# Attention beside a mixture of experts on one core: choice weights at step 70, block experts ten steps behind the slots, pairs sent at two places of a step, biases as bf16 rows of the projection

## The chip, the cores and the metric

The kernel runs on one core of one Trainium2 chip. Five engines work side by side, each through its own instructions in order: PE (TensorE, matmuls; its weight loads are shown as PEld), DVE (VectorE), ACT (ScalarE), POOL (GpSimd) and SP (which issues DMAs). The metric is the device time of one execution in microseconds (us), the median over several; lower is better.

## The reference

Input x is 8 x 512 tokens of 128 features. Both branches read the layer-normed x, and the output is their sum with x:

```python
xn = layernorm(x)
# attention, 16 heads of 8
h = xn @ W1 + b1                       # q, k, v
w = softmax(causal(q k^T / sqrt(8)))
attn = (w @ v) @ Wp + bp
# mixture of 8 experts, 2 per token, and one shared
logits = xn @ gate_w.T
topw, topi = top_k(softmax(logits), 2)
topw = topw / (topw.sum(-1) + 1e-20)
ffn(x, g, u, d) = silu(x @ g.T) * (x @ u.T) @ d.T     # 352 wide
moe = ffn(xn, shared) + sum over i of topw[i] * ffn(xn, expert[topi[i]])
out = x + attn + moe
```

## The kernel before

PE, DVE, ACT and SP work in the order in which the program was written; only POOL's instructions are put in order by a scheduler. The main loop (L1153) goes over 32 groups of four heads (eight batches of four groups), with five tiles of scores each: 160 steps. A step fills one PSUM tile with scores (`fill`, L315, single-buffered), takes the exponential on ACT (`weigh`, pT L443, 128x1024), and looks seven tiles ahead (`look`, L740): PE computes raw scores into two PSUM banks (sc_diag, sc_left, L365) and DVE reduces them to row maxima (peaks L394, L400), which are turned (mT L423, L425) and written by DMA as rows beside the queries. In `MORE` = steps 0, 12, 18, 24 the step looks twice, the second time at its end (L1182). Where `prepare` (L350) ran before a look, ACT has copied the causal mask into sc_diag (L353); where it has not, PE adds it by a matmul of 128x512 bf16 (L378).

Beside the scores, each step runs pieces of the expert network (`chunk`, L600): gu matmuls (L611), tanh on ACT (L616), two DVE operations that end in the gated h (L617, L618), and later the down projection y (L638). Shared blocks of 256 tokens come first (13 of them, to step 41), then 36 blocks of routed pairs, then the last shared ones. A shared block adds its y to x_sb on DVE (L648); a routed one copies it on ACT (o L644) and POOL scatters it (results L622).

Routing runs inside the same steps, one piece of the generator `route` (L907) per step from step 0 on: maxima of the logits and the places of all 8192 token-choice pairs (slot L986, step 5), the expert of each block (L991 to L998, step 6), and the choice weights (L1005 to L1023, step 7). From step 5, `send_some` (L682) issues two indirect DMAs per step on POOL (slots L690), each moving 128 rows to their slots; both wait for the exponential of their step. There are 64, and the slots are first loaded at step 40 and used at step 41. The weights are first used when the routed results are added, after step 148.

`offset` (L526) adds the sum of projected v bias and bp (bias_sb, made in `whole_bias`, L517) to a batch's x_sb on POOL (L529, 128x512), eight times in all. `join` (L533) projects a batch's attention with four fp32 matmuls (p_ps L537) and adds it to x_sb (L541). Two PSUM buffers named "mi" are shared in turn by all small results: v_ps, mT_ps, y, s_ps, ot, p_ps and others, so a new one waits until the one before the last has been read.

The order within a step, from the loop:

```python
waiting.append((kind, j, weigh(n, kind, j, on_pool)))
parts_then = look(step)
some_chunks(step, False)
...
parts_then()
if step not in MORE and len(looked) < total_steps:
    prepare(*divmod(len(looked), NTILES))
some_routing()
send_some()
```

Of the kernel before, what the change touches and what calls it, by code (L numbers as in the profile page):

```python
# [11 lines left out]
F32 = mybir.dt.float32  # L12
I32 = mybir.dt.int32
BF16 = mybir.dt.bfloat16
# [11 lines left out]
P = 128  # L26
# [26 lines left out]
AT_ONCE = 2  # L53
SENT = 2
LAG = 2
# [10 lines left out]
def attn_moe_kernel(  # L66
# [34 lines left out]
    bp_sb = const.tile([P, E], F32, name="bp_sb")  # L101
    bias_sb = const.tile([P, E], F32, name="bias_sb")

    def load_x(b):
# [91 lines left out]
    rows = rows_attT[:, :, :E]  # L196
    attT = rows
    weight = const.tile([P, TOPK, NT], F32, name="weight")
    slot = const.tile([P, TOPK, NT], I32, name="slot")
# [236 lines left out]

    last_exp = []

# [86 lines left out]

    def offset(b):  # L526
        xb = x_sb[:, ts(b, NC), :]
        with tc.issue_after(sent[-1]) if sent else ExitStack():
            nc.gpsimd.tensor_tensor(  # L529
                xb, xb, bias_sb.unsqueeze(1).to_broadcast([P, NC, E]), ALU.add  # L530
            )

    def join(b):  # L533

        ps = misc([P, NC, E], "p_ps")
        for c in range(NC):
            nc.tensor.matmul(  # L537
                ps[:, c], lhsT=attT[:, b * NC + c], rhs=wp_sb, start=True, stop=True
            )
        xb = x_sb[:, ts(b, NC), :]  # L540
        nc.vector.tensor_tensor(xb, ps, xb, ALU.add)  # L541
# [58 lines left out]
    def chunk(k, f):  # L600
# [16 lines left out]
        nc.vector.scalar_tensor_tensor(th, th, 1.0, gu[:, 0], ALU.add, ALU.mult)  # L617
        nc.vector.tensor_tensor(h[:, f], gu[:, 1], th, ALU.mult)  # L618

# [68 lines left out]
    def send(i, t):  # L688

        d = nc.gpsimd.indirect_dma_start(  # L690
            slots, bass.IndirectOffsetOnAxis(ap=slot[:, i, t : t + 1], axis=0),
            rows_attT[:, t, :], None,
        )
# [96 lines left out]
    nc.gpsimd.tensor_copy(count, count_i)  # L790
    logits = ro.tile([P, NT, NE], F32, name="logits")
    empty = ro.tile([P, WIPED, ROW], F32, name="empty")
# [114 lines left out]
    def route():  # L907

        rank_b = rank.unsqueeze(1).to_broadcast([P, NT, NE])
        lmax = ro.tile([P, NT], F32, name="lmax")  # L910
        nc.vector.tensor_reduce(lmax, logits, AX.X, ALU.max)
# [3 lines left out]
        for i in range(TOPK):  # L915
            if i:
                rest = ro.tile([P, NT, NE], F32, name="rest")
                nc.vector.scalar_tensor_tensor(rest, hots[0], MASKED, logits, ALU.mult, ALU.add)
                left = rest
                top = ro.tile([P, NT], F32, name=f"top{i}")  # L920
                nc.vector.tensor_reduce(top, left, AX.X, ALU.max)
# [65 lines left out]
        to_send.extend((i, t) for t in range(NT) for i in range(TOPK))  # L987
        yield

# [10 lines left out]
        )  # L1000
        yield


        prob = ro.tile([P, NT, NE], F32, name="prob")
        nc.vector.tensor_tensor(prob, logits, spread(lmax), ALU.subtract)  # L1005
        nc.scalar.activation(prob, prob, AF.Exp)
        psum = ro.tile([P, NT], F32, name="psum")
        nc.vector.tensor_reduce(psum, prob, AX.X, ALU.add)
        nc.vector.reciprocal(psum, psum)
        chosen = []  # L1010
        for i in range(TOPK):
            p_ = ro.tile([P, NT], F32, name=f"p{i}")
            nc.vector.tensor_tensor(p_, tops[i], lmax, ALU.subtract)
            nc.scalar.activation(p_, p_, AF.Exp)
            nc.vector.tensor_tensor(p_, p_, psum, ALU.mult)
            chosen.append(p_)
        wsum = ro.tile([P, NT], F32, name="wsum")
        nc.vector.scalar_tensor_tensor(
            wsum, chosen[0], 1e-20, chosen[1], ALU.add, ALU.add
        )  # L1020
        nc.vector.reciprocal(wsum, wsum)
        for i in range(TOPK):
            nc.vector.scalar_tensor_tensor(  # L1023
                weight[:, i], chosen[i], 0.5, wsum, ALU.mult, ALU.mult
            )

    routing = route()
    done_routing = []

# [81 lines left out]
    for t in range(FIRST):  # L1111
# [17 lines left out]
        if t == 3:  # L1129
            whole_bias()  # L1130
            offset(0)
        if t == 4:
# [20 lines left out]
    for n in range(B * NG):  # L1153
        b, g = divmod(n, NG)
        waiting = []
        for i, (kind, j) in enumerate(TILES):
# [13 lines left out]
            some_routing()  # L1170
            send_some()
            for f in late:
# [116 lines left out]
```

## Time and profile before

| what | us |
|---|---|
| three timed runs | 618.37, 620.67, 620.8 |
| median | 620.67 |
| the profiled execution | 616.3 |
| its span, first to last instruction | 614.6 |
| mean granted clock of PE | 0.968 of full |

The profile is of one execution. Its busy times are unions over an engine's instructions; an idle time is put down to whatever semaphore event came last before the waiting instruction. Matmul ends are modelled.

| group of instructions | count | mean ns |
|---|---|---|
| exponential, ACT L443, 128x1024 | 160 | 1026 |
| row maxima, DVE L394, 128x512 | 256 | about 684 |
| gu, PE L611, shared, 128x256 fp32 | 192 | 406 |
| mask into sc_diag, ACT L353 | 117 | 592 |
| mask matmul, PE L378, 128x512 bf16 | 11 | 381 |
| send of pairs, POOL L690 | 64 | 979 |
| bias added to x_sb, POOL L529 | 8 | 1271 |

Idle time of PE, DVE and ACT by what ended it is read from the list of waits; where in the run it falls, from the timeline.

### The profile page before, as it was taken

How to read it: one execution, taken by the hardware profiler on the slowest of the kernel's cores; microseconds unless marked ns; L12 is line 12 of the kernel's file. 1: busy time of each engine (PE TensorE's matmuls, PEld its weight loads, DVE VectorE, ACT ScalarE, POOL GpSimd, SP SyncE). 2: the span in 40 equal slices, each digit the busy share in tenths (PEclk: the TensorE clock that was granted, in tenths of full speed). 3: DMA queues.
4: the chain of work that ended last, by engine and by line, in shares of the span. 5: the costliest groups of instructions: out<-in, count | busy, mean ns of one | idle time of the engine just before them, and what ended most of it. 6: DMA issues, size and time to landing. Idle time of an engine off the chain costs nothing.

```text
span 614.6 us, 13602 instructions
## 1 busy us (share of the span) xinstructions
PE 563.3 (92%) x4796; PEld 414.0 (67%) x4796; DVE 463.3 (75%) x1213; ACT 370.4 (60%) x668; POOL 244.0 (40%) x365
## 2 busy tenths in 40 slices
PE   6989598798999999999999999999999999999964
PEld 4656375566666677777776877777777877786533
DVE  7787867676768787777787778687788778876594
ACT  5735354463547666686667666586667766665530
POOL 9510444643557234333433344233434334433320
PEclk9989799998999999999999999999999999999986
DMA  7744244142143674838585785838585875720471
GB/s 219 229 117 172 95 109 109 37 131 78 37 121 110 197 225 135 233 106 251 178 240 159 223 233 166 217 93 250 178 218 194 238 232 145 215 96 3 138 223 51
DMA packets 52363, 98.38 MB, mean 160 GB/s; under 512 B 10054, under 2 KB 35530, under 8 KB 50136
## 3 DMA queue, kind: packets, MB, share of 16 engines
q1 hardware_dynamic: 46216, 83.78, 47.6%
q0 software_dynamic: 5360, 13.66, 6.4%
q8 instruction: 38, 0.62, 0.4%
q14 instruction: 29, 0.24, 0.1%
q10 hardware_dynamic: 720, 0.08, 0.1%
HBM read 73.36 MB, written 24.26 MB: 159 GB/s over the span
## 4 chain that ended last, share of the span: by engine, by line
PE 67%; ACT 6%; DVE 6%; issue 2%; POOL 0%; ACTq 0%; DVEq 0%
PE gu L611 19%; PE av L466 11%; PE y L638 11%; PE scT L322 9%; PE sc_diag L365 5%; PE sc_left L365 4%; DVE x_sb L719 3%; ACT pT L443 2%; PE qk_ps L239 2%; ACT sc_diag L353 2%; PE p_ps L537 1%; ACT th L616 1%; PE s_ps L585 1%; PE aT_ps L514 1%; PE mT_ps L423 1%
## 5 line engine op out<-in xcount | busy, mean ns | idle before, releaser
L443 ACT ACTIVATE pT<-scT 128x1024 f32<-128x1024 f32 x160 | 164.1, 1026 | 68.6 <-PE scT L322 27.3
L622 POOL DMA_INDIRECT results<-o,goes x72 | 73.1, 1015 | 129.7 <-ACT o L644 110.0
L451 POOL TENSOR_SCALAR_AFFINE_SELECT pT<-pT 128x256 f32<-128x256 f32 (+1 forms) x168 | 72.4, 447 | 118.7 <-ACT pT L443 115.6
L611 PE MATMUL gu<-sT,w 128*128 128x128 f32 x864 | 116.0, 277 | 2.3 <-PE sc_left L365 0.8
L394 DVE TENSOR_REDUCE peaks<-sc_diag 128x4 f32<-128x512 f32 x128 | 88.0, 688 | 38.1 <-PE sc_diag L365 25.7
L611 PEld LDWEIGHTS gu<-sT,w 128*128 128x128 f32 x864 | 108.0, 191 | 6.8 <-PE sc_diag L365 1.8
L322 PE MATMUL scT<-qs,ks 75*128 75x384 bf16 (+3 forms) x512 | 103.2, 303 | 3.9 <-ACT pT L443 3.8
L690 POOL DMA_INDIRECT slots<-rows_attT,slot x64 | 62.6, 979 | 81.2 <-issue 36.2
L616 ACT ACTIVATE th<-gu 128x256 f32<-128x256 f32 x156 | 59.8, 384 | 57.7 <-PE gu L611 39.7
L466 PE MATMUL av<-pT,v_ext 128*32 128x512 f32 (+3 forms) x1024 | 91.2, 452 | 1.0 <-POOL pT L451 1.0
L365 PEld LDWEIGHTS <-qs 72*128 72x128 bf16 x896 | 64.9, 98 | 38.8 <-issue 20.6
L617 DVE SCALAR_TENSOR_TENSOR th<-th,gu 128x256 f32<-128x256 f32 x156 | 65.1, 417 | 32.7 <-ACT th L616 30.5
L394 DVE TENSOR_REDUCE peaks<-sc_left 128x4 f32<-128x512 f32 x128 | 87.1, 680 | 0.0
L353 ACT CAST sc_diag<-mask_q 128x512 f32<-128x512 bf16 x117 | 69.2, 592 | 25.3 <-DVE peaks L394 17.9
L365 PE MATMUL sc_diag<-ks,qs 72*128 72x128 bf16 (+1 forms) x576 | 62.1, 225 | 12.4 <-ACT sc_diag L353 11.0
L618 DVE TENSOR_TENSOR h<-gu,th 128x256 f32<-128x256 f32 x156 | 66.2, 424 | 5.4
L638 PEld LDWEIGHTS y<-w,h 128*128 128x128 f32 x432 | 54.2, 191 | 23.4 <-issue 10.6
L638 PE MATMUL y<-w,h 128*128 128x128 f32 x432 | 64.4, 285 | 1.2 <-ACT v_ext L289 1.2
L365 PE MATMUL sc_left<-ks,qs 72*128 72x128 bf16 (+1 forms) x320 | 61.7, 274 | 3.2 <-DVE peaks L394 3.1
L322 PEld LDWEIGHTS <-ks 75*128 75x128 bf16 x512 | 46.8, 99 | 23.7 <-issue 12.5
L611 PE MATMUL gu<-xnT,ws_sb 128*128 128x256 f32 x192 | 54.1, 406 | 3.3 <-DVE h L618 3.2
L466 PEld LDWEIGHTS av<-pT,v_ext 128*32 128x32 f32 x1024 | 23.6, 109 | 32.2 <-issue 21.6
(166 smaller groups left out, 634.5 us busy)
## 6 DMA issues: line engine op xcount, KB each, us to landing
w<-in_w_exp_dram SPq DMA_DIRECT2D x72, 576.0 KB
qs<-dq SPq DMA_DIRECT2D x45, 192.0 KB
ks<-dk SPq DMA_DIRECT2D x45, 192.0 KB
slots<-empty POOLq DMA_DIRECT2D x6, 780.0 KB
s<-slots SPq DMA_DIRECT2D x33, 130.0 KB
r<-results SPq DMA_DIRECT2D x16, 256.0 KB
dq<-parts SPq DMA_DIRECT2D x7, 384.0 KB
dk<-parts SPq DMA_DIRECT2D x7, 384.0 KB
```

Of the source, the lines that this page charges most:

```text
L322: nc.tensor.matmul(out_, lhsT=k[: QK + 3, ts(i, P)], rhs=q[: QK + 3, i * P :], start=True, stop=bare)
L353: nc.scalar.copy(diag_ps.rearrange("p (b k) -> p b k", k=P), mask_q.unsqueeze(1).to_broadcast([P, NC, P]),)
L365: nc.tensor.matmul(out_, lhsT=q[:QK, ts(c, P)], rhs=k[:QK, keys], start=start, stop=stop, skip_group_check=True,)
L394: nc.vector.tensor_reduce(peaks[:, i, 8 + 4 * t : 12 + 4 * t], banks[t].rearrange("p (b k) -> p b k", k=P), AX.X, ALU.max,)
L443: last_exp[:] = [nc.scalar.activation(pT, ps, AF.Exp, scale=D**-0.5).ins]
L451: nc.gpsimd.affine_select(out=d, in_=d, pattern=[[0, d.shape[1]], [1, P]], compare_op=ALU.is_ge, fill=0.0, base=0, channel_multiplier=-1,)
L466: nc.tensor.matmul(av[32 * jj : 32 * jj + 32, c * P :], lhsT=v_ext[b % NV][:, c, 4 * g + jj, :], rhs=weights, start=(n % 2 == 0 and c == 0 ...
L611: nc.tensor.matmul(gu[:, i, part], lhsT=w[c][:, ds(i * FP + f * P, P)], rhs=sT[:, part], start=True, stop=True,)
L616: nc.scalar.activation(th, gu[:, 0], AF.Tanh, scale=0.5)
L618: nc.vector.tensor_tensor(h[:, f], gu[:, 1], th, ALU.mult)
L622: d = nc.gpsimd.indirect_dma_start(results, bass.IndirectOffsetOnAxis(ap=goes_of[k][:, c : c + 1], axis=0), o, None, bounds_check=NP - 1, ...
L638: nc.tensor.matmul(y, lhsT=h[:, f, ts(c, P)], rhs=w[c % len(w)][:, ds(2 * FP + f * P, P)], start=(f == 0), stop=(f == NF - 1),)
```

## The change

Five edits. The block experts follow the slots by ten steps (`EXPERTS_AT`), at step 15. The choice weights become a generator of their own, run from step 70 to 73 (`WEIGHTS_AT`), with their inputs (logits, maxima) kept in buffers that live through the kernel. Of the two sends of a step the second is issued at its end and waits for the gated h of the step's chunk instead of the exponential. In steps 13, 19 and 25 the chunk stands ahead of the look, and the mask is no longer prepared by ACT for them. `offset` goes; the sum of biases is split into three bf16 parts, each kept on one row of a 128x128 tile, and a matmul with ones adds these rows in `join`.

```diff
-SENT = 2
+EXPERTS_AT = 10
+WEIGHTS_AT = 70
...
     def whole_bias():
...
+        part = ln.tile([P, 3, E], BF16, name="bias_part", bufs=1)
+        for i in range(3):
+            nc.gpsimd.tensor_copy(part[:, i], bias_sb)
+            if i < 2:
+                nc.gpsimd.tensor_tensor(bias_sb, bias_sb, part[:, i], ALU.subtract)
+            nc.gpsimd.tensor_scalar(
+                part[:, i], part[:, i], ident[:, i : i + 1], None, ALU.mult
+            )
+        nc.gpsimd.tensor_tensor(bias16, part[:, 0], part[:, 1], ALU.add)
+        nc.gpsimd.tensor_tensor(bias16, bias16, part[:, 2], ALU.add)
-    def offset(b):
-        xb = x_sb[:, ts(b, NC), :]
-        with tc.issue_after(sent[-1]) if sent else ExitStack():
-            nc.gpsimd.tensor_tensor(
-                xb, xb, bias_sb.unsqueeze(1).to_broadcast([P, NC, E]), ALU.add
-            )
     def join(b):
...
-                ps[:, c], lhsT=attT[:, b * NC + c], rhs=wp_sb, start=True, stop=True
+                ps[:, c], lhsT=attT[:, b * NC + c], rhs=wp_sb, start=(c == 0), stop=False,
+                skip_group_check=True,
             )
+        nc.tensor.matmul(
+            ps, lhsT=ones16, rhs=bias16.unsqueeze(1).to_broadcast([P, NC, E]),
+            start=False, stop=True, skip_group_check=True,
+        )
...
-        nc.vector.tensor_tensor(h[:, f], gu[:, 1], th, ALU.mult)
+        last_gate[:] = [nc.vector.tensor_tensor(h[:, f], gu[:, 1], th, ALU.mult).ins]
...
-    def send_some():
-        for _ in range(SENT):
-            if to_send:
-                send(*to_send.pop(0))
+    def send_one(behind):
+        if to_send:
+            send(*to_send.pop(0), behind)
...
-        tc.add_manual_dep(d.ins, last_exp[0].name, SYNC, reason="in their step")
+        tc.add_manual_dep(d.ins, behind.name, SYNC, reason="in their step")
...
         to_send.extend((i, t) for t in range(NT) for i in range(TOPK))
-        yield
+        for _ in range(EXPERTS_AT):
+            yield
...
+    def weigh_choices():
+        nc.vector.tensor_tensor(logits, logits, spread(best[0]), ALU.subtract)
+        nc.scalar.activation(logits, logits, AF.Exp)
+        chosen = best[2:]
+        for p_, top in zip(chosen, best):
+            nc.vector.tensor_tensor(p_, top, best[0], ALU.subtract)
+            nc.scalar.activation(p_, p_, AF.Exp)
         yield
-        prob = ro.tile([P, NT, NE], F32, name="prob")
-        nc.vector.tensor_tensor(prob, logits, spread(lmax), ALU.subtract)
-        nc.scalar.activation(prob, prob, AF.Exp)
...
+        nc.vector.tensor_reduce(best[1], logits, AX.X, ALU.add)
+        nc.vector.reciprocal(best[1], best[1])
+        yield
+        for p_ in chosen:
+            nc.vector.tensor_tensor(p_, p_, best[1], ALU.mult)
...
+        yield
...
             whole_bias()
-            offset(0)
...
-            parts_then = look(step)
-            some_chunks(step, False)
+            if step - 1 in MORE:
+                some_chunks(step, False)
+                parts_then = look(step)
+            else:
+                parts_then = look(step)
+                some_chunks(step, False)
...
             some_routing()
-            send_some()
+            if step >= WEIGHTS_AT:
+                next(weighing, None)
+            send_one(last_exp[0])
...
             some_chunks(step, True)
+            send_one((last_gate or last_exp)[0])
+            last_gate.clear()
             if step in MORE:
                 look(step)()
-                prepare(*divmod(len(looked), NTILES))
...
-        if n % NG == 2 and b + 1 < B:
-            due(step + 1, partial(offset, b + 1))
```

On the engines' orders this means: PE gains eight bias matmuls (and two mask matmuls, in steps 13 and 25), ACT loses two mask copies, POOL gains ten small operations in the preamble and loses eight additions, DVE's instructions are the same and stand elsewhere, and SP's order is the same.

More of the change, by code (lines that the diff above doesn't have):

```diff
@@ L102, in attn_moe_kernel @@
     bias_sb = const.tile([P, E], F32, name="bias_sb")
+    bias16 = const.tile([P, E], BF16, name="bias16")
     def load_x(b):
@@ L197, in attn_moe_kernel @@
     attT = rows
+    logits = const.tile([P, NT, NE], F32, name="logits")
+    best = []
+    for i in range(2 * TOPK):
+        t = const.tile([P, NT], F32, name=f"best{i}")
+        best.append(t)
     weight = const.tile([P, TOPK, NT], F32, name="weight")
@@ L435, in put_shift @@
             )
-    last_exp = []
+    last_exp, last_gate = [], []
     def weigh(n, kind, j, on_pool):
@@ L680, in attn_moe_kernel, with send @@
     to_send = []
-    def send_some():
-        for _ in range(SENT):
-            if to_send:
-                send(*to_send.pop(0))
-    def send(i, t):
+    def send_one(behind):
+        if to_send:
+            send(*to_send.pop(0), behind)
+    def send(i, t, behind):
         d = nc.gpsimd.indirect_dma_start(
@@ L790, in attn_moe_kernel @@
     nc.gpsimd.tensor_copy(count, count_i)
-    logits = ro.tile([P, NT, NE], F32, name="logits")
     empty = ro.tile([P, WIPED, ROW], F32, name="empty")
@@ L909, in route @@
         rank_b = rank.unsqueeze(1).to_broadcast([P, NT, NE])
-        lmax = ro.tile([P, NT], F32, name="lmax")
+        lmax = best[0]
         nc.vector.tensor_reduce(lmax, logits, AX.X, ALU.max)
@@ L919, in route @@
                 left = rest
-                top = ro.tile([P, NT], F32, name=f"top{i}")
+                top = best[i]
                 nc.vector.tensor_reduce(top, left, AX.X, ALU.max)
@@ L1000, in route @@
         )
-        yield
-        prob = ro.tile([P, NT, NE], F32, name="prob")
[L1005 to L1017, printed above, removed]
+    def weigh_choices():
[5 more added lines that the diff above has]
+            nc.scalar.activation(p_, p_, AF.Exp)
+        yield
+        nc.vector.tensor_reduce(best[1], logits, AX.X, ALU.add)
[3 more added lines that the diff above has]
+            nc.vector.tensor_tensor(p_, p_, best[1], ALU.mult)
         nc.vector.scalar_tensor_tensor(
-            wsum, chosen[0], 1e-20, chosen[1], ALU.add, ALU.add
+            best[0], chosen[0], 1e-20, chosen[1], ALU.add, ALU.add
         )
-        nc.vector.reciprocal(wsum, wsum)
+        yield
+        nc.vector.reciprocal(best[0], best[0])
         for i in range(TOPK):
             nc.vector.scalar_tensor_tensor(
-                weight[:, i], chosen[i], 0.5, wsum, ALU.mult, ALU.mult
+                weight[:, i], chosen[i], 0.5, best[0], ALU.mult, ALU.mult
             )
     routing = route()
+    weighing = weigh_choices()
     done_routing = []
```

## The prediction

> **What bounds the kernel now.** I read the page first, then the sums by stretch, the waits of PE, and the timeline at each wait. "Step" is one pass of the inner loop, found in the trace by its exponential (pT L443, 160 of them).
>
> ```profile
> PE 563.3 (92%) x4796; PEld 414.0 (67%) x4796; DVE 463.3 (75%) x1213; ACT 370.4 (60%) x668; POOL 244.0 (40%) x365
> ...
> 61.00:85.40 24.40, 17.90 (x120) 12.54 (x119) 17.29 (x49) 9.46 (x20) 10.25 (x10) 0.79 0.42 116
> 85.40:126.00 40.60, 34.88 (x287) 23.95 (x286) 29.48 (x74) 21.05 (x34) 20.67 (x21) 1.00 0.24 66
> ...
> 201.00:304.30 103.30, 99.92 (x909) 77.06 (x906) 81.22 (x205) 69.81 (x131) 38.05 (x62) 1.00 0.66 194
> ```
>
> In a row by stretch, the first pair is start:end, then length, busy time of PE, PEld, DVE, ACT, POOL, then the granted clock. From 201 us on PE is busy 97%: that stage is bound by PE's own instructions. From 61 to 126 us (steps 6 to 19) PE idles 12.2 of 65 us, and in the first part its clock is 0.79. That early stage is what can be won. Its waits, from the timeline (start, duration, engine, line, and in brackets the idle time before it and what ended it):
>
> ```profile
> 71.76 0.42 ACT L1006 ACTIVATE prob<-prob 128x256 f32<-128x256 f32 x1 [1.13 <-DVE prob L1005]
> ...
> 73.68 0.23 ACT L1014 ACTIVATE p<-p 128x32 f32<-128x32 f32 x1 [0.36 <-DVE p L1013]
> 73.81 0.63 ACT L289 COPY v_ext<-v_ps 128x256 f32<-128x256 f32 x2
> ...
> 74.50 1.65 PE L638 MATMUL y<-ws_sb,h 128*128 128x128 f32 x6 [3.43 <-ACT v_ext L289]
> ...
> 97.39 0.38 PE L365 MATMUL sc_diag<-ks,qs 72*128 72x128 bf16 x4 [1.80 <-ACT sc_diag L353]
> ...
> 121.19 0.38 PE L365 MATMUL sc_left<-ks,qs 72*128 72x256 bf16 x2 [1.54 <-DVE peaks L394]
> ...
> 147.30 0.38 PE L365 MATMUL sc_diag<-ks,qs 72*128 72x128 bf16 x4 [2.22 <-ACT sc_diag L353]
> ```
>
> The choice weights (L1005 to L1025) bounce between DVE and ACT; the v copy queued behind them on ACT comes 2.9 us after its v_ps ended (70.90), and PE stands 3.43 us for the buffer. The other three waits are in the steps after those that look twice (MORE: 12, 18, 24). Two waits lie elsewhere:
>
> ```profile
> 102.87 0.97 POOL L690 DMA_INDIRECT slots<-rows_attT,slot  x1 [0.30 <-issue]
> ...
> 104.89 1.02 ACT L443 ACTIVATE pT<-scT 128x1024 f32<-128x1024 f32 x1 [2.64 <-PE gu L611]
> 104.93 0.69 DVE L400 TENSOR_REDUCE peaks<-sc_left 128x2 f32<-128x512 f32 x1 [1.77 <-PE gu L611]
> ...
> 205.12 1.27 POOL L529 TENSOR_TENSOR x_sb<-x_sb,bias_sb 128x512 f32<-128x512 f32 x1 [2.71 <-DVE second L588]
> 205.13 1.27 DVE L592 SCALAR_TENSOR_TENSOR goes<-second,s 128x2 int32<-128x2 f32 x1
> ```
>
> ACT and DVE start together at 104.9, though PE had issued the scores they need by 103.3: what PE finished was told late. It is 1.0 us after the end (103.84) of the last of four indirect sends in a row (99.03, 100.30, 101.59, 102.87). The same holds for the rows of four that end at 94.82 and 144.72 (DVE's x_sb L648 starts at 95.82 and 145.74). I read it as: after four sends back to back PE's signals are held for about 1 us; rows of two show no clear hold.
>
> **What the Trainium skill says.** "TensorE: Matmul & The Clock Gate", What's actually happening: PE's clock is full or half, decided over windows of about 3.4 us of activity. The trace agrees: PE is at half clock from 72.9 to 79.7 and 148.0 to 151.4, each right after an idle of 3.43 and 2.22 us; idles of 1.8 us and less brought none. "SBUF — State Buffer", SBUF: two separate sides: GpSimd and VectorE share a port pair as an exclusive lock, and a VectorE operation with two SBUF inputs waits for the whole GpSimd one. The trace agrees: goes L592 (mean 193 ns) took 1.27 us beside the POOL addition of the same length. On sends that hold PE's signals I found no page.
>
> **The change part by part**, against the profiled execution (span 614.6 us, 616.3 in all). The median of the three timed runs is 620.67, 4.4 above it; I take the differences over to the median.
>
> *Weights to steps 70 to 73, experts ten steps later.* Step 6 loses four DVE instructions (66.73 to 68.61: 1.9 us), step 7 eleven on DVE and three on ACT (71.31 to 75.1). Re-laying ACT and DVE there: parts L254 starts at 66.85, the reductions at 67.7, the v copy at 70.95 when v_ps is done, so y L638 starts at 71.65 instead of 74.50: 2.85. With an idle of 0.6 instead of 3.43 the half-clock window goes too; PE's work from 74.5 to 79.9 then takes 5.4 - 2.6. By the end of step 8's gu I get 74.8 for 79.92: **-5.0** (-2.9 if the half clock stays). Next late is again the ACT copy of the mask, 0.3 as before. In step 15 the experts' 1.9 us land on DVE at 108.1, where DVE stood idle for 2.1 us waiting on POOL's offset (x_sb L648, 110.23), so they take that gap.
>
> At step 70 (304.3) the cost comes back in a PE-bound stage: DVE gets three operations after h (306.9), ACT three exponentials behind them, ahead of o_sb, sT and the next exponential. Laid out, ACT is free at about 308.3, so o_sb starts 1.9 us late, PE's ot waits 0.8 for it, and the next scores 0.35 for the exponential: **+1.2**. Steps 71 to 73 add only DVE work of 0.5 to 0.8 us before waits of 0.6 to 1.2. Bounds 0 and +2.1 (the whole ACT delay).
>
> *Chunk before look in steps 13, 19, 25, no mask copied for them.* gu (0.9 to 1.03) runs in the wait; in 13 and 25 the mask comes as a matmul (L378, next instruction 0.22 later) instead of an ACT copy of 0.59. Without a held signal as well, the reductions are done when gu is: step 13 -1.8 + 0.2 = **-1.6**, step 19 **-1.0**, step 25 -2.2 + 0.2 = **-2.0**, and its half-clock window, 3.4 us, goes: **-1.7**.
>
> *Sends at two places.* The second now waits for the gate (h L618) of its step. Laying the 64 sends out by the ends of exponentials and gates in this trace, rows of four in steps 8 to 27 vanish (longest there three); some remain at steps 30 to 36, where the present ones cost PE little (0.7 at 174.5, 0.8 at 182.9). Gain in step 15: DVE's chain runs from 103.4, x_sb at 108.8 for 110.23: **-1.4** (-0.2 if the hold stays). Steps 28 to 35: **-0.5** (0 to -1.5). Behind a waiting send stand on POOL only later sends; the last one ends where it did (190.3 in both layouts), and the loads of slots behind them lose three offsets of 1.27.
>
> *Biases in the projection.* Eight POOL additions go; one of them held goes L592 1.1 us and through ACT's v copy PE's s_ps (wait 1.37 at 208.3): **-1.05**. Eight matmuls of 128x512 bf16 come, at the 0.22 us of L378's form: **+1.8** (0 if they fall in waits; 3.0 at the 381 ns each takes alone). At the start ten POOL operations of 128x128 stand at 29 to 33 us, some with two SBUF inputs, beside DVE's small m_parts chain; with the fetch landing late anyway I take **+0.3** (0 to +1).
>
> Sum: -5.0 - 1.6 - 1.0 - 3.7 - 1.4 - 0.5 - 1.05 = -14.25; +1.2 + 1.8 + 0.3 = +3.3; together **-11.0**. All of the gain lies before the PE-bound stage, which then starts earlier; the SP order is the same, weights and slots are triggered by step, and the row maxima that SP loads for the scores have 6.5 us or more from issue to use (95.97 to 102.44, the shortest after step 6). So 605.3 for the profiled execution, and 609.7 for the median, 610 rounded.
>
> **Rivals.**
> A (0.60): as laid out, 610; own range 606 to 614.
> B (0.22): the send layout doesn't help, because gate and next exponential come close together and rows of four persist in other steps. For it: the steps get shorter, and gate to exponential is often under 1.27 us. Against: my layout. Then step 13 gives 0.8, step 15 0.2, step 25 2.5, the late part 0: -7.3, 613.4.
> C (0.11): the early stage is refilled: another wait, DVE's (busy 71 to 73% there) or the fetches of q and k, takes the freed time, and of 14.25 only some 5 remain: -1.7, 619.
> D (0.07), slower: the exchange in steps 70 to 73 and the bias matmuls at their high ends (2.1 + 3.0 + 1 = 6.1) while the second send, waiting at the head of POOL's queue for gates, delays the last slots. Today these loads are issued at 197.1 to 199.4 and first used by PE at 203.4. From about 3 us of delay on, PE stands at step 41, each such idle of over 2.2 us brings a half-clock window, and it decides once more than 8 us are lost there. Then 624. Against it: the layout ends at the same place.
>
> **Numbers.** Three us (0.5%) is about what a measurement of this kernel tells from no change. Faster by more (under 617.6): all of A and B and a little of C, 0.84; the same: most of C, 0.09; slower: D, 0.07. Range 605.5 to 616.5: A and B with the bounds of the half clock (2.1), the late sends (1.0) and step 70 (1.2), C and D left out.
>
> **What would show it.** Weights: no ACT wait at L1006's place, y L638 of step 7 within 1 us of v_ps, clock of the stretch from 69 to 80 us at 1.0. Chunks: no wait over 0.6 us before sc_diag in steps 13 and 25. Sends: no start of ACT and DVE together 1 us after a fourth send. Bias: matmuls of 128x512 bf16 0.22 apart. Step 70: ot waiting for o_sb by 0.5 to 1.5 us. Wrong if PE idles as much before 200 us as now, or if slots come late at step 41.

## The result, and the profile after

The changed kernel took 610.28 us (median of 4 runs, 609.00 to 612.92), the kernel before 619.52 (4 runs, 617.86 to 620.8; three of them are the runs shown before the prediction): ratio 0.9858, 95% interval 0.9813 to 0.9902, a gain of 6.1 to 11.6 us. Some executions have a lower clock and lie over 1.5% above the fastest of their kernel; the medians here and below count them and the ratios leave them out, so a ratio need not be the quotient of its medians. The profiled execution of the changed kernel took 609.89 us with a span of 608.2; that of the kernel before had 616.3 and 614.6.

First the engines' totals and the sums by stretch of the changed kernel (start:end, length, then busy time of PE, PEld, DVE, ACT, POOL, the granted clock, DMA share and GB/s):

```profile
PE 564.8 (93%) x4806; PEld 412.0 (68%) x4806; DVE 460.8 (76%) x1213; ACT 368.2 (61%) x666; POOL 236.9 (39%) x367
...
61.00:80.00 19.00, 15.36 (x117) 10.37 (x116) 13.55 (x35) 9.25 (x17) 9.57 (x10) 0.91 0.46 127
80.00:119.00 39.00, 36.03 (x298) 24.96 (x297) 30.98 (x79) 20.29 (x33) 19.43 (x21) 1.00 0.29 79
...
191.00:294.00 103.00, 100.68 (x914) 77.73 (x913) 80.45 (x205) 69.78 (x131) 35.55 (x60) 1.00 0.65 195
```

The two early stretches cover the same steps (6 to 19) as before. They are 58 us long for 65, PE idles 6.6 us in them for 12.2, and the clock of the first has gone from 0.79 to 0.91. The PE-bound stage is as full as it was.

Now the waits that the prediction had named, from the timeline of the changed kernel (start, duration, engine, line, in brackets the idle time before it and what ended it):

```profile
72.31 0.94 PE L655 MATMUL y<-ws_sb,h 128*128 128x128 f32 x6 [0.57 <-ACT v_ext L297]
...
94.24 0.38 PE L373 MATMUL sc_diag<-ks,qs 72*128 72x128 bf16 x4 [0.65 <-ACT sc_diag L361]
...
107.95 0.96 POOL L706 DMA_INDIRECT slots<-rows_attT,slot  x1 [0.30 <-issue]
...
109.83 0.69 DVE L402 TENSOR_REDUCE peaks<-sc_diag 128x4 f32<-128x512 f32 x1 [2.35 <-PE gu L628]
...
114.72 0.38 PE L373 MATMUL sc_left<-ks,qs 72*128 72x256 bf16 x2 [1.54 <-DVE peaks L402]
...
139.04 0.39 PE L373 MATMUL sc_diag<-ks,qs 72*128 72x128 bf16 x4
...
161.69 0.96 POOL L706 DMA_INDIRECT slots<-rows_attT,slot  x1 [0.30 <-issue]
...
163.87 1.02 ACT L451 ACTIVATE pT<-scT 128x1024 f32<-128x1024 f32 x1 [2.95 <-PE gu L628]
```

Step 7's wait for the copy of v fell from 3.43 to 0.57 us. Of the waits after a double look, that of 1.80 in step 13 and that of 2.22 in step 25 (139.04 has no bracket) are gone; the 0.65 at 94.24 stands one step later, at the look of step 14, whose mask ACT still copies. That of 1.54 at step 19 is there as before. The last send shown ends a row of four at 162.65, and ACT's exponential starts 1.2 us after it: PE's signals are still held, here and at 108.91, where a row of three ended. ("Held" means that ACT or DVE starts late on something that PE had finished.)

One wait that the prediction did not list is as long as before and now the longest of this stage: at 66.41 in the changed kernel, ahead of the look of step 7, PE stands 2.79 us for ACT's copy of the mask (2.78 in the kernel before), and a half-clock window follows, from 67.0 to 70.4. e7 and f2 below try to shorten it.

The table follows the start of the exponential step by step, changed minus before, in us, as what each stretch of steps added. The first column is this pair of traces; the second is the pair e6 and e5 below, from a chip on which the kernel before takes 609 us.

| steps | first pair | e5 minus e6 |
|---|---|---|
| to 5 | +0.69 | +0.01 |
| 6 to 9 | -5.38 | -4.55 |
| 10 to 14 | -1.35 | -0.19 |
| 15 to 19 | -1.19 | +0.33 |
| 20 to 24 | +0.43 | -0.33 |
| 25 to 27 | -3.68 | -0.60 |
| 28 to 41 | +0.75 | 0.00 |
| 42 | -1.06 | -1.07 |
| 43 to 69 | +0.45 | +0.46 |
| 70 to 73 | +0.89 | +0.89 |
| 74 to 159 | +4.4 | -2.3 |

The last row is no work of the change except the 0.21 to 0.25 us of each of four projections before the last steps. In the first pair the rest stands from step 148 on, beside half-clock windows (before 588 to 592 and 599 to 602, after 555 to 559 and 582 to 589); in the second, 2.97 of it stand at step 130, in a half-clock window that e6 alone has, from 499 to 503. These windows differ between executions of one kernel. "TensorE: Matmul & The Clock Gate" of the Trainium skill, What's actually happening, calls the window free-running and what it costs run-variable; these traces agree: the changed kernel's second trace (e5) has none between 71 and 592 us.

### The profile page after: what moved, and what is told of

The parts are those of the page before. It is cut to its first block, busy times and chain, and to the rows that moved or that the text cites. A ratio compares the mean times of both kernels' runs of the same rounds, so it can differ in the third digit from the quotient of the medians.

```text
span 608.2 us, 13658 instructions
## 1 busy us (share of the span) xinstructions
PE 564.8 (93%) x4806; PEld 412.0 (68%) x4806; DVE 460.8 (76%) x1213; ACT 368.2 (61%) x666; POOL 236.9 (39%) x367
## 4 chain that ended last, share of the span: by engine, by line
PE 76%; DVE 9%; ACT 8%; issue 3%; DMA 2%; SPq 0%; POOL 0%; ACTq 0%; DVEq 0%; POOLq 0%
PE gu L628 21%; PE av L474 12%; PE y L655 12%; PE scT L330 10%; PE sc_diag L373 6%; PE sc_left L373 5%; ACT pT L451 3%; DVE x_sb L735 3%; PE qk_ps L247 2%; ACT sc_diag L361 2%; DVE peaks L402 2%; ACT th L633 2%; PE p_ps L549 1%; PE s_ps L602 1%; DVE h L635 1%
## 5 line engine op out<-in xcount | busy, mean ns | idle before, releaser
L639 POOL DMA_INDIRECT results<-o,goes x72 | 72.9, 1012 | 131.4 <-ACT o L661 110.0
L330 PEld LDWEIGHTS <-ks 75*128 75x128 bf16 x512 | 46.6, 99 | 23.5 <-issue 12.2
```

Of the source, the lines that this page charges most:

```text
L330: nc.tensor.matmul(out_, lhsT=k[: QK + 3, ts(i, P)], rhs=q[: QK + 3, i * P :], start=True, stop=bare)
L639: d = nc.gpsimd.indirect_dma_start(results, bass.IndirectOffsetOnAxis(ap=goes_of[k][:, c : c + 1], axis=0), o, None, bounds_check=NP - 1, ...
```

## The experiments

Times are medians of 6 to 22 runs; ratios are to the kernel before, run on the same chip. e1 to e4 ran on one chip, e5 to e8 on a second, f1 to f3 on a third and g1 on a fourth, each on one occasion; which chip the first pair ran on is not on record.

**e1, both sends at one place.** The changed kernel with

```diff
             send_one(last_exp[0])
+            send_one(last_exp[0])
...
-            send_one((last_gate or last_exp)[0])
-            last_gate.clear()
```

> The changed kernel, but both sends of a step stand at one place behind the exponential, as before the change. Theory (rows of four sends back to back hold PE's signals for about 1 us): rows of four come back in steps 8 to 27; exponentials start later than in the changed kernel by 0.8 at step 13, 1.2 more at step 15 and 0.5 to 2.5 more at step 25; in all +2 to +4.5 us, ratio to the kernel before 0.989 to 0.993. Rival (the place of the second send doesn't matter, the hold follows the number of sends that fall near each other in any layout): within 1 us of the changed kernel, ratio 0.985 to 0.987, and no new wait of PE over 0.5 us in steps 8 to 27.

604.92 us, ratio 0.9914 (0.9889 to 0.9939). But the kernel before, 619.5 the first time, took 610.33 here, and the ratios expected for e1 to e4 were worked out from 619.5. So I compare these four with e5 below, the changed kernel beside a kernel before of 609.37; that e1's ratio lies in the theory's range says nothing. By the ratios e1 is 0.7 us slower than e5 (the two intervals leave -1.6 to 2.9). In the timeline of e1 the rows of four are back, and nothing is held:

```profile
142.14 0.96 POOL L706 DMA_INDIRECT slots<-rows_attT,slot  x1 [1.69 <-ACT pT L451]
...
145.93 0.95 POOL L706 DMA_INDIRECT slots<-rows_attT,slot  x1 [0.31 <-issue]
...
146.90 0.22 PE L334 MATMUL scT<-mask_k,ident 128*128 128x128 bf16 x1
...
147.21 1.02 ACT L451 ACTIVATE pT<-scT 128x1024 f32<-128x1024 f32 x1 [2.22 <-PE scT L334]
```

The row ends at 146.88, the last score matmul at 147.12, and the exponential starts 0.09 us after that. In the first profiles it would have come at about 147.9. The waits expected at steps 13, 15 and 25 are absent. Against e5 below, the exponentials of e1 differ by at most 0.1 us in every stretch from step 6 to 73. So the rival is nearer, though for another reason than it gave: rows are there, yet a row need not hold anything. What the one place costs where signals are held was not run.

**e2, weights and experts back in steps 6 and 7.** The changed kernel with

```diff
-        for _ in range(EXPERTS_AT):
-            yield
+        yield
...
+        yield
+        yield from weigh_choices()
...
-            if step >= WEIGHTS_AT:
-                next(weighing, None)
```

> The changed kernel, but the choice weights are worked out in step 7 and the experts of the blocks in step 6 again. Theory: the wait of PE of 3.4 us at step 7 and the half-clock window behind it come back, exponentials start 5.0 us later from step 9 on; steps 15 to 17 lose up to 0.5 less or more, since the experts' 1.9 us leave step 15; steps 70 to 73 win 0.9 to 1.2; in all +3.8 to +4.5, ratio to the kernel before 0.992 to 0.994. Rival (the early stage refills: what step 7 loses is taken back by shorter waits in steps 8 to 25): +0 to +1.5, ratio 0.986 to 0.988.

608.11 us, ratio 0.9967 (0.9942 to 0.9991). From its timeline, the exponentials on ACT at the head of the copy of v that PE waits for:

```profile
71.16 0.42 ACT L1023 ACTIVATE logits<-logits 128x256 f32<-128x256 f32 x1 [1.13 <-DVE logits L1022]
...
73.08 0.23 ACT L1030 ACTIVATE best<-best 128x32 f32<-128x32 f32 x1 [0.36 <-DVE best L1029]
73.22 0.63 ACT L297 COPY v_ext<-v_ps 128x256 f32<-128x256 f32 x2
...
73.90 1.44 PE L655 MATMUL y<-ws_sb,h 128*128 128x128 f32 x5 [3.48 <-ACT v_ext L297]
```

The wait is 3.48 us again, and the half-clock windows behind it stand from 72.6 to 79.5. By the ratios e2 is 3.9 us slower than e5; 3.8 to 4.5 were expected. Against e5 the exponentials lose 5.51 us in steps 6 to 9, win 1.27 in steps 15 to 19, where the experts' instructions are gone, and 0.89 in steps 70 to 73. The theory holds at each of its places; in steps 15 to 19 e2 wins more than the 0.5 it allowed.

**e3, look ahead of chunk again in steps 13, 19, 25.** The changed kernel with

```diff
-            if step - 1 in MORE:
-                some_chunks(step, False)
-                parts_then = look(step)
-            else:
-                parts_then = look(step)
-                some_chunks(step, False)
+            parts_then = look(step)
+            some_chunks(step, False)
...
                 look(step)()
+                prepare(*divmod(len(looked), NTILES))
```

> The changed kernel, but in steps 13, 19 and 25 the look stands ahead of the chunk again, and ACT prepares their mask. Theory (the order of look and chunk takes the waits ahead of the diagonal scores): the wait at step 13 comes back with 0.8 to 1.2 us, that at step 25 with 1.0 to 2.2, and if it is over 2 us a half-clock window worth 1.7 with it; step 19 doesn't change; in all +2 to +4, ratio 0.989 to 0.992. Rival (the waits were those of the held signals, which the sends took away): +0 to +0.8, ratio 0.986 to 0.987, and no wait over 0.8 us at steps 13 and 25.

607.99 us, ratio 0.9966 (0.9944 to 0.9988). The three waits in the timeline of e3:

```profile
92.33 0.38 PE L373 MATMUL sc_diag<-ks,qs 72*128 72x128 bf16 x4 [0.73 <-ACT sc_diag L361]
...
114.40 0.38 PE L373 MATMUL sc_left<-ks,qs 72*128 72x256 bf16 x2 [1.54 <-DVE peaks L402]
...
139.24 0.38 PE L373 MATMUL sc_diag<-ks,qs 72*128 72x128 bf16 x4 [0.72 <-ACT sc_diag L361]
```

Where nothing is held, look first waits 0.73 us at step 13 and 0.72 at step 25, not 1.80 and 2.22; that is the rival's bound. Against e5 the order costs 0.56 each after steps 19 and 25 (in the exponentials of steps 20 and 25) and nothing net at step 13, since e5 waits 0.65 for ACT's mask in step 14 instead. By the ratios e3 is 3.8 us slower than e5 (the two intervals leave 1.7 to 5.9), more than the 1.2 us that these waits show. Its trace has a longer half-clock window before step 9 besides, which I can't lay to the order, so the size of this part is not settled.

**e4, biases by POOL again.** The changed kernel with

```diff
+    def offset(b):
+        xb = x_sb[:, ts(b, NC), :]
...
+            nc.gpsimd.tensor_tensor(
+                xb, xb, bias_sb.unsqueeze(1).to_broadcast([P, NC, E]), ALU.add
+            )
...
-        nc.tensor.matmul(
-            ps, lhsT=ones16, rhs=bias16.unsqueeze(1).to_broadcast([P, NC, E]),
-            start=False, stop=True, skip_group_check=True,
-        )
```

> The changed kernel, but the biases are added to x by POOL again (eight additions of 1.27 us), and the projections have no bias matmul and the preamble no split of the biases. Theory: each projection after the early steps is shorter by 0.21 to 0.22 us, in all -1.8; the preamble is shorter by 0.3 to 0.7; the wait of PE at step 41 behind a held goes comes back with +1.05, and at step 15 x_sb waits for POOL again, 0 to +1.4: in all -1.4 to +0.3, ratio 0.9835 to 0.986. Rival (the additions on POOL delay sends and slots, which is what the bias rows are worth): +1 to +3, ratio 0.988 to 0.991.

605.90 us, ratio 0.9953 (0.9927 to 0.9978), by the ratios 3 us over e5's: the upper end of the rival's +1 to +3, and none of the theory's. Two places of its timeline, POOL's additions and what stood beside them:

```profile
100.15 1.49 DVE L417 TENSOR_TENSOR row_max<-peaks 128x12 f32<-128x12 f32 x1
...
100.31 1.29 POOL L537 TENSOR_TENSOR x_sb<-x_sb,bias_sb 128x512 f32<-128x512 f32 x1
...
102.40 0.75 DVE L998 TENSOR_TENSOR done<-count,ends 128x576 f32<-128x576 f32 x1
...
192.58 1.27 POOL L537 TENSOR_TENSOR x_sb<-x_sb,bias_sb 128x512 f32<-128x512 f32 x1 [2.71 <-DVE second L596]
192.60 1.27 DVE L600 SCALAR_TENSOR_TENSOR goes<-second,s 128x2 int32<-128x2 f32 x1
...
195.72 0.44 PE L593 MATMUL s_ps<-ident,s 128*128 128x128 f32 x2 [1.36 <-ACT v_ext L297]
```

At 100 us a maximum of 0.16 us takes 1.49 beside the addition, and the experts' instructions (L998 and on, 1.9 us) follow at once: PE waits 1.74 us for a buffer that DVE empties behind them, a half-clock window follows (105.0 to 108.4), and steps 15 to 19 lose 2.26 us against e5. At step 42 the wait of 1.36 costs 1.07. Each projection is 0.22 shorter, as expected. Neither theory had the first of these: what the addition costs there is DVE's time beside it, not POOL's queue. "SBUF — State Buffer" of the Trainium skill, SBUF: two separate sides, says that GpSimd and VectorE share a port pair as an exclusive lock. Both pairs of lines agree in that DVE's operation ends with the addition (101.64 beside 101.60, 193.87 beside 193.85). The page also gives the pair to whichever starts first; by the recorded starts DVE was 0.16 us ahead in the first pair and ended with the addition all the same.

**e5 and e6, both kernels again on one chip.** No edit.

> The changed kernel itself, a second time, for a comparison on one chip. The kernel before took 619.5 us beside it the first time and 610.3 beside e1 to e4, whose traces show no signal of PE held after a row of sends. Theory A (the hold comes and goes from chip to chip, whatever the kernel): if the kernel before takes about 610 here, the traces have no quiet of PE's signals after a row of sends, the changed kernel's waits at steps 30 to 36 are gone (4 us less before step 38 than in its first profile), step 19 waits 0.6 us in place of 1.54, and its time is 603 to 606 us, ratio 0.989 to 0.993: less than the 0.986 of the first time, as the kernel before has lost its holds too. Theory B (the hold belongs to the kernel's own layout of sends): the waits at steps 30 to 36 are there again, as in the first profile, with the time near 609.

> The kernel before, unchanged, for its trace on the chip of this call. Theory A (holds come and go from chip to chip): where the time is about 610, the rows of four sends are in POOL's timeline as before, but ACT's exponential and DVE's reduction start as soon as their scores are written; the waits of PE at steps 13, 25 and at about 174 and 183 us are under 0.9 us each, and there is no half-clock window at step 25; the wait of 3.4 us at step 7 stays. Theory B (a row of four always holds): the waits of 1.8, 1.5 and 2.2 us at steps 13, 16 and 25 are there again.

603.64 us (ratio 0.9903, 0.9876 to 0.9930) and 609.46 us (1.000, 0.9979 to 1.0021). Neither trace has a stretch without signals of PE that ends after a row of sends. A count over all the traces, of exponentials before 320 us, gives two groups: in e1 to e8 and g1 none starts more than 0.15 us after its scores are done and ACT is free; more than 0.35 us late are 8 in the first trace of the kernel before, 7 in the changed kernel's, 10 in f1, 12 in f2 and 3 in f3. From the timeline of e6, the kernel before, with a row of four that ends at 141.23:

```profile
138.99 0.97 POOL L690 DMA_INDIRECT slots<-rows_attT,slot  x1 [0.30 <-ACT pT L443]
140.26 0.97 POOL L690 DMA_INDIRECT slots<-rows_attT,slot  x1 [0.30 <-issue]
...
141.27 0.68 DVE L394 TENSOR_REDUCE peaks<-sc_diag 128x4 f32<-128x512 f32 x1
...
142.62 0.38 PE L365 MATMUL sc_diag<-ks,qs 72*128 72x128 bf16 x4 [0.72 <-ACT sc_diag L353]
```

and from that of e5:

```profile
108.24 0.69 DVE L402 TENSOR_REDUCE peaks<-sc_diag 128x4 f32<-128x512 f32 x1 [0.78 <-PE sc_diag L373]
...
113.62 0.38 PE L373 MATMUL sc_left<-ks,qs 72*128 72x256 bf16 x2 [0.61 <-DVE peaks L402]
```

In e6 the reduction starts at once after the row, and step 25 waits 0.72 us where it waited 2.22. The line of e5 at 108.24 is the reduction that the changed kernel's first trace has at 109.83: from 104 us up to there the two traces run within 0.02 us of each other, with the same three sends from 105.4 to 108.9, and in the first the signal comes 1.6 us later. (For the copy of v, step 7 waits 2.15 us in e6, not the 3.4 expected, and 3.44 in g1.) The same kernel's first trace is later by 9.3 us over steps 10 to 41 (+1.30, +1.69, +3.07 and +3.20 in steps 10 to 14, 15 to 19, 25 to 27 and 28 to 41), the changed kernel's first trace by 5.0, of which 3.95 in steps 28 to 41. I take these sums as an estimate of what the held signals cost each of them, the half-clock window behind step 25 included. Theory A stands as far as the two layouts go: the hold does not belong to the kernel. Whether it belongs to the chip or to the occasion is not shown, since each chip was used once. Step 19's wait of 0.61 shows what the new order does there when no signal is held.

**e7, one place, weights smoothed, chunk ahead of the look in step 6.** As e1, and

```diff
-WEIGHTS_AT = 70
+WEIGHTS_AT = 72
...
+        yield
         nc.scalar.activation(logits, logits, AF.Exp)
+        yield
+        for p_ in chosen:
+            nc.scalar.activation(p_, p_, AF.Exp)
...
-            if step - 1 in MORE:
+            if step - 1 in MORE or step == 6:
...
```

> The changed kernel with three edits: both sends at one place behind the exponential as in e1; the choice weights from step 72 on, with their exponentials one and two steps behind the subtractions, so that none of them stands ahead of o_sb; the chunk ahead of the look at step 6 too, with the mask there by a matmul. Theory: one place is worth 0 to 2 us where nothing is held; steps 70 to 73 win 0.7 to 0.9 against the changed kernel; at step 6 the wait of 2.6 to 2.8 us for the mask copied by ACT becomes 1.2 to 1.7, and its half-clock window goes with it (another 1.7): in all 3 to 5 us faster than the changed kernel of the same call. Rival (the early stage refills): the wait at step 6 is as long, or step 7 waits as much more, and only the 0.9 of steps 70 to 73 is left.

604.49 us, ratio 0.9927 (0.9900 to 0.9955): no faster than e5. Steps 70 to 73 win the whole 0.89 (the exponential of 71 comes 1.42 us earlier). PE's wait ahead of the look of step 7 is not shorter, 3.20 us for 2.78 in e5: I had set the edit one step early, since PE has already filled step 7's scores when it stands, so that the look in question is step 7's.

**e8, the weights' part alone.** The kernel before with the first part of the change (`weigh_choices` as in the change):

```diff
-        yield
+        for _ in range(EXPERTS_AT):
+            yield
...
+            if step >= WEIGHTS_AT:
+                next(weighing, None)
             send_some()
```

> The kernel before with the first part of the change alone: experts ten steps behind the slots, choice weights from step 70. Theory: exponentials start 5.0 to 5.5 us earlier than in the kernel before from step 9 on, steps 15 to 18 give 1 to 2 of them back where the experts' five operations land on DVE, and steps 70 to 73 cost 0.9: in all -2.5 to -4 us, ratio 0.9935 to 0.996. Rival (refilled): steps 8 to 25 give back all but 1 us, ratio 0.998 to 1.001.

607.23 us, ratio 0.9946 (0.9917 to 0.9976), in the theory's range for the whole. Its profiled execution (611.8 us) lies above its median, so I take from the trace only where the time was given back. Against e6 that is 4.3 us in steps 15 to 19, two half-clock windows from 109.0 to 115.8 included, more than the 1 to 2 expected. The timeline at step 16:

```profile
104.28 1.86 DVE L424 TENSOR_TENSOR m_parts<-m_rest,m_parts 128x16 bf16<-128x16 f32 x1
...
104.82 1.28 POOL L536 TENSOR_TENSOR x_sb<-x_sb,bias_sb 128x512 f32<-128x512 f32 x1
...
108.19 0.21 PE L430 MATMUL mT_ps<-ident,m_parts 128*48 128x128 bf16 x1 [2.16 <-DVE x_sb L655]
```

It is e4's place: DVE's small operation for 1.86 us, to the end of the addition beside it (recorded as starting 0.54 us after it), then the experts, and PE waiting for m_parts. So the experts' move and the bias rows belong together: ten steps on, the experts meet a POOL addition unless it has gone.

**f1, f2, f3, on a chip where the kernel before takes 619.37 us.** f1 is the changed kernel. f2 smooths the weights as e7, sets the chunk first in step 7 and gives POOL the biases from batch 3 on. f3 sends eight pairs a step at one place, and nothing at the second. The first two pieces are f2's, the last is f3's:

```diff
-            if step - 1 in MORE:
+            if step - 1 in MORE or step == 7:
...
+        if n % NG == 2 and 3 <= b + 1 < B:
+            due(step + 1, partial(offset, b + 1))
...
-            send_one(last_exp[0])
+            for _ in range(8):
+                send_one(last_exp[0])
...
-            send_one((last_gate or last_exp)[0])
-            last_gate.clear()
```

> The changed kernel once more, as the mark for f2 and f3 on the chip of this call. If the hold is a matter of the chip: either no quiet of PE's signals after a row of sends and a time of 603 to 605 us with the kernel before at 609 to 611 (as on the chips of e1 to e8), or the quiets of the first profile with 609 to 611 beside 619 to 621. Anything else (holds with 603, none with 610) would speak against reading the difference of the two pairs of times as the hold's.

> The changed kernel, both places of sends kept, with three edits. Weights from step 72 on, exponentials one and two steps behind the subtractions: steps 70 to 78 win 0.9 against the changed kernel. Chunk ahead of the look in step 7, its mask by a matmul: theory, the wait there falls from 2.8 us to 1.0 to 1.7 and its half-clock window goes, 1.5 to 3.0 us earlier by step 9; rival, VectorE has no free time there (its slots, parts and reductions stand back to back) and the wait goes on to its next reduction: 0 to 0.7. Biases by POOL for the batches from 3 on, by the matmul for 0 to 2: the projections from step 64 on lose 0.21 us each, 1.05 in all, with no new wait at steps 17 and 42. Together 3 to 5 us faster than the changed kernel of this call, 2 if the rival holds.

> The changed kernel with eight sends a step, all behind the exponential, so that POOL issues all 64 in one row of about 80 us, from about 62 us on. Theory A (on this chip sends hold nothing): no quiet of PE's signals over 1.5 us within the row or after it, exponentials within 1.5 us of the changed kernel at step 40, time within 2 us of it. Theory B (a row holds from some length on, longer on some chips): from some send of the row on, PE's signals come in bunches, every wait for PE grows by 1 us and more, and the exponentials of steps 8 to 30 start 5 us and more later, time 609 or more.

f1: 612.89 us, 2 to 4 us over the time expected, ratio 0.9876 (0.9847 to 0.9906), a gain of 5.8 to 9.5 us. The kernel before is at 619 again and the held signals are there again, for example behind a row of four that ends at 86.84, with scores done by 85.4:

```profile
85.88 0.96 POOL L706 DMA_INDIRECT slots<-rows_attT,slot  x1 [0.39 <-issue]
...
87.75 1.03 ACT L451 ACTIVATE pT<-scT 128x1024 f32<-128x1024 f32 x1 [2.57 <-PE gu L628]
```

f3: 673.54 us, ratio 1.0894 (1.0839 to 1.0949), 61 us over f1. Its sends stand in three rows, of 24, 24 and 16. The first runs from 63.6 to 93.92; PE ended mT_ps at 72.46, y at 75.69 and the scores for the next exponential at 76.97:

```profile
74.45 1.24 PE L655 MATMUL y<-ws_sb,h 128*128 128x128 f32 x6 [1.99 <-ACT v_ext L297]
75.16 0.22 DVE L433 COPY mT<-mT_ps 48x128 bf16<-48x128 bf16 x1 [4.12 <-remote]
...
82.54 0.29 DVE L665 SCALAR_TENSOR_TENSOR x_sb<-y,x_sb 128x128 f32<-128x128 f32 x1 [7.16 <-remote]
...
92.96 0.96 POOL L706 DMA_INDIRECT slots<-rows_attT,slot  x1 [0.31 <-issue]
...
97.35 1.02 ACT L451 ACTIVATE pT<-scT 128x1024 f32<-128x1024 f32 x1 [22.95 <-remote]
...
98.42 0.37 PE L330 MATMUL scT<-qs,ks 75*128 75x256 bf16 x1 [19.42 <-ACT pT L451]
```

DVE's copy of mT_ps starts 2.7 us after it was done, DVE's use of y 6.9 us, and the exponential 20 us after its scores and 3.4 us after the row. So what PE finished is told during a row too, but ever later as the row goes on. Theory B, and by far more than expected. It is an edit of the sends alone, on the same chip as f1, that makes the signals late; f3 has not run on a chip of the other sort.

The number of sends in a row is not all that counts. The first row, five sends from 62.9 to 69.2 in the changed kernel's first trace, held nothing: ACT and DVE start within 0.04 us of their times in e5 there. And an exponential of the kernel before is 0.8 us late at 184.4 behind a row of two.

f2: 612.75 us, ratio 0.9895 (0.9849 to 0.9941), no better than f1. Smoothing gave its 0.90. The wait ahead of the look of step 7 is replaced by one of 2.95 us, now of gu for the gated h of the chunk ahead: VectorE is full there, which is the rival. And step 42 lost 1.07 again: POOL's additions for later batches were all issued by step 44, one of them beside goes at step 41.

**g1, the two places of sends alone.** The kernel before with the send functions of the change and nothing else:

```diff
-            send_some()
+            send_one(last_exp[0])
...
             some_chunks(step, True)
+            send_one((last_gate or last_exp)[0])
+            last_gate.clear()
```

> The kernel before with one part of the change alone: of the two sends of a step the second stands at the step's end and waits for the gated h. Two sorts of chip have been seen: on one the kernel before takes 609 to 610 us and no signal of PE is held after sends, on the other 619 to 620 us and they are. Theory (the second place is worth what it takes away of the holds): on a chip of the first sort nothing, within 1.5 us of the kernel before, ratio 0.998 to 1.002; on a chip of the second sort 2 to 4 us less, ratio 0.9935 to 0.997, with fewer or shorter quiets of PE's signals before step 28 than the kernel before has. Rival (rows of four only move to other steps): on the second sort too within 1.5 us, with as many quiets in other places.

608.62 us, ratio 0.9988 (0.9969 to 1.0007); the kernel before took 609.65, and no signal is held in its trace: there the second place is worth nothing, as expected. On a chip with holds this part has not run alone.

## Why the prediction was right, point by point

The time (610 for 610.28) and the direction came as forecast. That the two times are so close is in part luck: the forecast took 11.0 us off 620.67, and the medians give 9.2 off 619.52. The interval of the first measurement, 6.1 to 11.6 us, holds rival A's 11.0 and rival B's 7.3 alike; that of f1, the same kernel again beside a kernel before of 619.37, holds B's and leaves A's out. And f1 has rows of four at 82, 89 and 97 us, which is what rival B said: they only move. So the layout of the sends was worth less than forecast, and not the same each time.

Part of the forecast rests, besides, on a condition I did not see: I read from one trace that rows of four sends hold PE's signals, and on three chips, whose traces I have for the same or nearly the same kernels, they do not. There the change is worth about 6 us (ratio 0.9903), again nearer to rival B's 7.3.

- **Weights and experts, -5.0.** -5.38 and -4.55 by step 9, half-clock window included; e2 gives it back with 5.51. Right in place and size. "They take that gap" for the experts' 1.9 us in step 15 leaned on a gap that held signals and the addition had made, and the change takes the addition away; in e2 against e5 the experts cost 1.27 there.
- **Chunk before look, -1.6, -1.0, -2.0 and -1.7 for the window.** In the first pair steps 13 and 14 gave 2.1 us (step 12 lost 0.7) and step 25 with the next 3.7 as forecast, step 19 nothing. What I had called the wait of the order was mostly the held signal, as far as the two sorts of chip show: without holds the kernel before waits 0.73 and 0.72 us in steps 13 and 25, and the order is worth 0 there in the one and about 0.6 in the other. At step 19 the term of -1.0 failed in the first trace because a row of three sends ended just before and held the reductions (109.83 for e5's 108.24); without holds it gave 0.9 of wait (1.54 to 0.61).
- **Sends at two places, -1.4 and -0.5.** "Rows of four in steps 8 to 27 vanish" held in the first trace, though rows of three held signals as well, and step 15 won its 1.44 there, which step 16 lost and step 17 won again; in f1 rows of four are back and hold signals from 82 to 102. The second part failed: the rows that remain at steps 30 to 36 do not "cost PE little". Against e5 they cost the changed kernel 3.95 us in steps 28 to 41, about what they cost the kernel before (3.20), so nothing was won. I had priced them by PE's idle time at two places instead of comparing whole steps.
- **Biases, -1.05 and +1.8.** Step 42 gave 1.06 and each projection cost 0.21 to 0.22: both right. Missing is the addition's collision with DVE in steps 15 to 19 once the experts are there, which e4 prices at 2.26, its half-clock window included.
- **Steps 70 to 73, +1.2.** +0.89, within the bounds, and e7 shows it to be the weights' exponentials ahead of o_sb. It was the next exponential that came late; ot waited only 0.17 us.
- **The start, +0.3.** +0.69 in the first pair, +0.01 in e5 against e6; the kernel before itself differs by 1.4 us at the first exponential between its two traces. Not separable.
- **The end.** I carried no change past step 73 but the projections. The changed kernel's profiled execution lost 3.5 us after step 147 against that of the kernel before, beside half-clock windows. The latter lay 3.2 us under its median, the former 0.4, so the two profiled executions differ by 6.4 us and the medians by 9.2.

What stays open: why PE's signals are held during rows of indirect sends on some chips, or on some occasions, and not on others; and, where they are held, how much of the gain in steps 10 to 27 (about 5.8 us in the first pair) is the chunk's new place and how much the sends', since e1, e3 and g1 ran where nothing is held.

## What to carry to other kernels

A wait seen in one trace may belong to the chip or the occasion: repeat the trace of the old kernel on another chip before pricing its removal, and split an edit's worth by whether the wait is there. Work moved to an idle place needs a look at what else is due there on the other engines; here the experts cost 1.27 us in steps 15 to 19 without POOL's addition (e2 against e5) and 2.26 more with it (e4). It is worth keeping rows of indirect DMAs on POOL short: two places a step cost nothing where nothing is held (g1), and rows of 24 and 16 made this kernel 9% slower than the kernel before where signals are held (f3). That two places gain where signals are held is not shown.

## What the runs showed of the hardware

- Where signals of PE were held, they came about 1 us after the end of a row of three or four indirect sends (0.91 us in f1, 0.92 and 1.2 at 108.91 and 162.65 of the changed kernel's first trace). In a row of 24 they came 2.7, 6.9 and 20 us late. The first row, five sends to 69.2 in that first trace, held nothing. On other chips rows of four held nothing: the exponential followed its scores by 0.09 us (e1).
- The kernel before took 609 to 610 us on three chips and 619 to 620 on a fourth and in the first measurement; the steps in which signals were held, a half-clock window behind one of them included, make 9.3 us of that between two traces.
- A half-clock window followed an idle of PE of 1.74 us (e4), shorter than the 1.80 that the prediction had found harmless. In the trace of the kernel before, the half-clock windows that start at 66.1, 72.9, 148.0 and 588.3 us are 2, 22 and 129 times 3.41 us apart, so I count in windows of this grid: e4's 1.74 fall inside one (101.6 to 105.0), while the 1.80 of the kernel before are cut at 96.8, 1.2 us before and 0.6 after.
- VectorE operations of 0.16 to 0.19 us took 1.27, 1.49 and 1.86 us beside one POOL addition of 1.27 to 1.29, and each ended within 0.05 us of its end.
